# A graph stage in which the centres ride in spare rows, layer two's outputs come out turned, and one more round lies behind the scores

## The chip, the cores and the metric

The kernel runs on one core of a Trainium2 chip. The metric is the time of one execution on the device in microseconds; a kernel is timed several times and its median is given. A profile of one more execution shows what each engine did: PE is TensorE (PEld its weight loads), DVE is VectorE, ACT is ScalarE, POOL is GpSimd, SP issues the DMAs. L with a number is a line of the kernel before.

## The reference, cut to what matters

The whole program has three stages that follow each other: a graph stage (two graph convolutions and a projection), a state-space scan, and a small feed-forward stage. The change lies in the graph stage alone.

There are 16 graphs (`B`) of 512 nodes with 32 features. Four sort orders of the nodes (Morton and Hilbert keys of their coordinates) give each node four windows of 10 neighbours. A graph convolution is:

```python
gf = concatenate([center, neigh - center])       # per sort order, 10 neighbours each
x16 = stack(per order)[..., perm].reshape(B*N, 10, 256).astype(float16)
qh = x16.reshape(B*N, 10, 8, 32)                  # eight heads of 32
attn = softmax(einsum(qh, qh) / sqrt(32))         # 10 x 10 for each node and head
fused = (attn @ qh) @ W_lin.T + b_lin             # 64 channels
h = lrelu(instance_norm(W_conv @ fused))          # 32 channels in layer one, 64 in layer two
feats_next = h.max over the 10 neighbours
```

The layer-one result feeds layer two, and both feed a projection `W_conv3`, whose output is normalized and added to `x`.

In the heads that hold only centres all ten rows of a node are equal, so attention leaves them as they are: they add the same vector to all ten outputs of a node. The kernel computes this "centre share" once per node, together with the biases, and the attention only for the four heads of differences.

## The kernel before, in words

The 16 graphs are handled four at a time (`g` = 0 to 3), on 128 partitions. One pass (`at`) is one layer of one such group; there are eight, in the order (0, layer 1), (1, layer 1), (0, layer 2), (2, layer 1), (1, layer 2), (3, layer 1), (2, layer 2), (3, layer 2). A pass has 43 rounds (`gi`), each for 12 nodes of every graph, so that there are 344 rounds. Queries and keys of three nodes lie in a block of 30 out of 32 columns; a round has four such blocks (`j`), four heads (`h`) and four graphs (`b`).

The steps of a block, each an instruction sequence on its own engine:

- `differences` (POOL, L827) writes neighbour minus centre into `DD`, six rounds ahead; every third round four DMAs on SP's queue copy it into the block-diagonal `DX` (L837).
- `scores` (PE, L862 and L869): a mask product over the whole bank, then 16 products into one PSUM bank `s` (two banks).
- `greatest` (DVE, L878) takes the maximum of each row; `expo` (PE L886, ACT L891) subtracts it by a product with an identity and takes the exponential.
- `sums`, `shares` (DVE L898 and L904, POOL L906): the sum, its reciprocal, and the normalized weights in `EN`. `turn` (DVE L912) transposes them in 32 x 32 blocks into `e`.
- `mapped` (PE L931, ACT L936): the differences through the combined weight `W_conv W_lin` into `us`. The weight is split into three bf16 parts `WA[0..2]`, so there are 48 matmuls a round with 128 (layer one) or 256 (layer two) columns. In layer two `us` takes two banks.
- `outputs` (PE L959): `us` and `e` make the convolution's output `h`, with channels on the partitions: 16 matmuls, `us` is the weight operand and 30 columns of `e` move. In layer one four rounds share the one bank `h`, and at the start of each four, one fp32 product of an identity with `hc` (the centre share, ten times over) lays the centre share into the bank (L949). In layer two, two rounds share a bank.
- `reduce`, `rest` (DVE L976, L982, L985): in layer two the centre share is added (L976), then maximum over the neighbours and moments for the normalization. After a pass, `end` normalizes (L1008 to L1021), and after layer two `finish` projects (L1030).

Beside the rounds run the rank comparisons (`rank_step`, PE L556 into a bank tagged `misc`, ACT L557 reads it), up to three a round in the first pass, one or two in the second and fourth, none in the others; and the preparation of the next pass (`prep`), cut into steps of which one or two are done per round: splitting features, the centre share (L682, L683), one-hot matrices (DVE L767) and their products that sort the features (PE L721, bank `pp`), then a store to memory (`dS`) and spread loads (`fs`, `crep`), all on SP's queue.

The order on every engine is written out by hand. The loop of rounds gives each step a lag: in iteration `it`, `expo` works on round `it-1`, `turn` on `it-3`, `scores` on `it`, `reduce` on `it-4`, `greatest` and `mapped` on `it`, `sums` and `shares` on `it-1`, `outputs` on `it-3`. [...] PSUM has eight banks: two for `s`, two for `u` (mapped products), one `h`, one `pp`, two `misc`.

Of the kernel before, what the change touches and what calls it, by code (L numbers as in the profile page):

```python
# [393 lines left out]
def graph_part(nc, tc, cx, I, dram, id32, ones, xt, F0, layernorm_steps, rstd_steps, scan_input):  # L394
# [45 lines left out]
    for L, co in ((1, 32), (2, 64)):  # L440
        WA = [gc.tile([P, 4, 4, co], BF16, name=f"WA{L}_{k}") for k in range(3)]
        WC = gc.tile([P, co // 32, P], F32, name=f"WC{L}")
        for t in (*WA, WC):
            zero(t)
        layers.append((L, co, co // 32, WA, WC, gc.tile([P, 1], F32, name=f"HB{L}")))

# [17 lines left out]
    for b in range(4):  # L464
        cols = slice(32 * b, 32 * b + 32)
        for j in range(2):
            nc.sync.dma_start(out=W3[cols, j, cols], in_=I["wc3T"][32 * j:32 * j + 32])
        nc.sync.dma_start(out=W3[64 * (b % 2):64 * (b % 2) + 64, 2 + b // 2, cols], in_=I["wc3T"][64:128])
# [22 lines left out]
    for t in (*DD, *EN):  # L491
        zero(t)

# [7 lines left out]
    def weights(L, co, npair, WA, WC, HB):  # L501
# [20 lines left out]
        for k in range(3):  # L522
            for b, rb in enumerate(rows):
                nc.scalar.copy(WA[k][rb, :, b], pw[rb])
            if k == 2:
                break
# [5 lines left out]
        for b in range(4):  # L532
# [3 lines left out]
        wt4 = wp.tile([64, P], F32, name=f"wtr{L}")  # L536
        nc.scalar.copy(
            wt4.rearrange("p (r o) -> p r o", o=co), wt.unsqueeze(1).to_broadcast([64, P // co, co])
        )
        pb = kps.tile([P, 1], F32, tag="w", name=f"pb{L}", bufs=2)  # L540
        nc.tensor.matmul(pb, lhsT=wt4, rhs=bl, start=True, stop=True)
        nc.scalar.copy(HB, pb)
# [84 lines left out]
    ps_s = cx.enter_context(tc.tile_pool(name="gps_s", bufs=2, space=PSUM))  # L627
# [8 lines left out]
    def later_tile(n):  # L636
        return ps_1.tile([P, D], F32, tag="misc", bufs=2, name=f"kd{n}")
# [5 lines left out]
    def prep(g, layer, early=False):  # L643
# [11 lines left out]
        pf = ps_1.tile([P, 4, P], F32, tag="misc", bufs=2, name=f"pf{key}")  # L655
# [14 lines left out]
        def share():  # L670
# [8 lines left out]
            hc = wk.tile([P, npair, D], F32, tag="hc", name=f"hc{key}")  # L679
            for pr in range(npair):  # L680
                ph = ps_1.tile([P, D], F32, tag="misc", bufs=2, name=f"ph{key}_{pr}")
                nc.tensor.matmul(ph, lhsT=WC[:, pr], rhs=c32, start=True, stop=True)  # L682
                nc.scalar.activation(hc[:, pr], ph, AF.Identity, bias=HB)  # L683
                yield
            made[key][2] = hc

        made[key] = [None, None, None]
# [4 lines left out]
        later = []  # L692
# [150 lines left out]
    def begin(at):  # L843
# [5 lines left out]
        mxo = wk.tile([P, npair, D], F32, tag="mxo", name=f"mxo{key}")  # L849
        stats = wk.tile([P, npair, nst, 6], F32, tag="stats", name=f"stats{key}")  # L850
# [63 lines left out]

    def mapped(at, gi):
# [3 lines left out]
        d = DD[slot]  # L919
        us = sm.tile([P, NJ, 4 * co], F32, tag="us", name=f"us{at}_{gi}", bufs=4)  # L920
        u = None
        nj = NJ // npair
        for j in range(NJ):
# [4 lines left out]
            for k in range(3):  # L928
                for h in range(4):
# [3 lines left out]
                        start=(jj == 0 and k == 0), stop=(k == 2), skip_group_check=True,  # L933
# [4 lines left out]

    def outputs(at, gi):
        key, co, npair, WA, hc, per = state[at][:6]  # L940
        us, e = live.pop(("us", at, gi)), live.pop(("e2", at, gi))
        slot = gi % per
        if slot == 0:
            live["h", at] = ps_1.tile([P, npair, per * NQ], F32, tag="h", name=f"h{at}_{gi}")
            if npair == 1:

                f0 = gi * NG
                nn = min(f0 + per * NG, D) - f0
                nc.tensor.matmul(  # L949
                    live["h", at][:, 0, :nn * K].rearrange("p (n j) -> p n j", j=K), lhsT=id32,  # L950
                    rhs=hc[:, 0, f0:f0 + nn].unsqueeze(2).to_broadcast([P, nn, K]), start=True, stop=False,
                    skip_group_check=True,
                )
        h = live["h", at]
        for j in range(NJ):
            for b in range(4):
                pr, r = divmod(b * co, P)
                q0 = slot * NQ + j * QB
                nc.tensor.matmul(  # L959
                    h[r:r + co, pr, q0:q0 + QB], lhsT=us[:, j, b * co:(b + 1) * co],  # L960
                    rhs=e[:, 4 * j + b, :QB], start=npair > 1, stop=True, skip_group_check=True,
                )
# [3 lines left out]
    def reduce(at, gi):  # L966
        key, co, npair, WA, hc, per, mxo, stats = state[at]
# [5 lines left out]
        hs = h[:, :, :nn * K].rearrange("p r (n j) -> p r n j", j=K)  # L973
        if layers[order[at][1]][0] == 2:
            t = sm.tile([P, npair, per * NG, K], F32, tag="hs", name=f"hs{at}_{gi}", bufs=1)
            nc.vector.tensor_tensor(  # L976
                t[:, :, :nn], hs, hc[:, :, f0:f0 + nn].unsqueeze(3).to_broadcast([P, npair, nn, K]), ALU.add,
            )
            hs = t[:, :, :nn]

        def greatest_of():
            nc.vector.tensor_reduce(mxo[:, :, f0:f0 + nn], hs, AX.X, ALU.max)  # L982

        def moments(pr):
            nc.vector.bn_stats(stats[:, pr, gi // per], hs[:, pr].rearrange("p n j -> p (n j)"))  # L985

        if npair == 1:
            greatest_of()
            moments(0)
        else:  # L990
# [10 lines left out]
    def end(at):  # L1001

        g, layer = order[at]
        key, co, npair, WA, hc, per, mxo, stats = state.pop(at)
# [814 lines left out]
```

## Time and profile before

| | us |
|---|---|
| median of three runs | 2255.77 |
| lowest and highest | 2254.24, 2265.24 |
| profiled execution, its own time | 2259.84 |
| span of its instructions | 2258.1 |
| first exponential to the last (344 rounds) | 114.1 to 1291.8 |

| engine | busy us | share of the span | instructions |
|---|---|---|---|
| PE | 2058.6 | 91% | 40533 |
| PE weight loads | 1272.5 | 56% | 40586 |
| DVE | 1792.6 | 79% | 3972 |
| ACT | 1132.6 | 50% | 2066 |
| POOL | 833.6 | 37% | 913 |

Busy time is the union of an engine's instructions, and the modelled end of a matmul overlaps the next one's start. So what a step costs PE is read from start to start in the timeline. "Issue" is idle time for which the profile shows no semaphore. A stretch of time can be cut into windows, and the busy time of each engine asked for in each; this is how the passes are compared.

### The profile page before, as it was taken

What the parts mean: (1) busy time and instruction counts of PE and PEld (TensorE: products, weight loads), DVE (VectorE), ACT (ScalarE), POOL (GpSimd) and SP (SyncE); (2) the same over time, 40 slices, a digit from 0 to 9 for tenths busy, and PEclk for the clock granted to TensorE, in tenths of its full rate; (3) what the DMA queues carried; (4) which work ended last, traced back from release to release, by engine and by line L of the source; (5) the groups of instructions that cost most, each with busy time, mean ns of one, the idle gap of its engine ahead of it and who ended that gap; (6) DMA issues with size and microseconds to landing.
All of it is one profiled execution on the core that took longest, in us unless ns stands there. A gap on an engine that the chain in (4) does not pass through costs nothing. (4 is left out here: it accounts for less than half of the span.)

```text
span 2258.1 us, 91857 instructions
## 1 busy us (share of the span) xinstructions
PE 2058.6 (91%) x40533; PEld 1272.5 (56%) x40586; DVE 1792.6 (79%) x3972; ACT 1132.6 (50%) x2066; POOL 833.6 (37%) x913
## 2 busy tenths in 40 slices
PE   5599898999888998889999969988999999999998
PEld 2255555777456775567777734445465564656443
DVE  8488797999988999989999964397968668685554
ACT  5686577556666554445555523343545445353521
POOL 2156656556556565565555400021112111020210
PEclk9899999999999999999999979999999999999999
DMA  1323233142242321422311122211221312113210
GB/s 45 78 65 79 53 74 73 42 87 49 52 88 47 75 61 41 90 50 62 74 36 43 31 63 61 85 58 44 86 75 38 103 47 75 66 47 94 52 38 19
DMA packets 126395, 138.25 MB, mean 61 GB/s; under 512 B 21051, under 2 KB 84261, under 8 KB 125997
## 3 DMA queue, kind: packets, MB, share of 16 engines
q1 hardware_dynamic: 125997, 132.37, 23.1%
q8 instruction: 319, 5.23, 1.0%
q14 instruction: 79, 0.65, 0.1%
HBM read 77.02 MB, written 12.85 MB: 40 GB/s over the span
## 5 line engine op out<-in xcount | busy, mean ns | idle before, releaser
L906 POOL TENSOR_TENSOR EN<-e,rz 128x480 f32<-128x480 f32 x344 | 342.5, 996 | 500.8 <-DVE rz L904 415.1
L931 PE MATMUL u<-WA,DD 128*32 128x128 bf16 (+1 forms) x16512 | 412.7, 247 | 29.1 <-issue 28.3
L936 ACT COPY us<-u 128x512 f32<-128x512 f32 x516 | 302.1, 587 | 153.3 <-PE u L931 137.8
L931 PEld LDWEIGHTS <-DD 128*32 128x32 f16 x16512 | 337.7, 97 | 52.5 <-issue 50.9
L891 ACT ACTIVATE e<-s,smc 128x480 f32<-128x480 f32 x344 | 227.7, 662 | 255.3 <-PE s L886 222.9
L827 POOL TENSOR_TENSOR DD<-fs,crep 128x480 f16<-128x480 f32 (+2 forms) x344 | 349.7, 1017 | 0.0
L959 PEld LDWEIGHTS h<-e,us 128*32 128x32 f32 (+1 forms) x11008 | 244.9, 125 | 136.0 <-issue 68.9
L959 PE MATMUL h<-e,us 128*32 128x30 f32 (+1 forms) x11008 | 278.1, 210 | 32.8 <-issue 15.0
L1393 POOL TENSOR_TENSOR ssq<-ssq,sq 128x512 f32<-128x512 f32 x56 | 79.5, 1419 | 580.4 <-ACT sq L1392 580.4
L878 DVE TENSOR_REDUCE c<-s 128x16 bf16<-128x480 f32 x344 | 220.6, 641 | 85.2 <-PE s L869 81.5
L1200 PE MATMUL ppg<-hT,wing 128*128 128x512 f32 x512 | 239.9, 612 | 0.0
L1213 DVE SCALAR_TENSOR_TENSOR cyh<-ppch,t_conv_w,cyh 128x496 f32<-128x496 f32 (+2 forms) x192 | 137.5, 716 | 119.8 <-ACT cyh L1207 115.3
L1200 PE MATMUL ppch<-hT,winch 128*128 128x512 f32 x512 | 230.9, 593 | 0.7 <-ACT gs L1288 0.7
L912 DVE STREAM_TRANSPOSE e<-EN 128x512 f32<-128x512 f32 x344 | 224.7, 653 | 0.0
L898 DVE TENSOR_REDUCE z<-e 128x16 f32<-128x480 f32 x344 | 219.6, 638 | 0.4 <-ACT e L891 0.4
L557 ACT ACTIVATE sgn<-kd 128x512 bf16<-128x512 f32 x256 | 153.1, 598 | 50.2 <-PE kd L556 35.0
L869 PEld LDWEIGHTS <-DD 128*32 128x32 f16 x5504 | 80.7, 96 | 157.5 <-issue 134.3
L767 DVE TENSOR_SCALAR oh<-it,rank 128x512 bf16<-128x512 f16 x512 | 156.4, 366 | 9.3 <-PE pp L721 9.3
L869 PE MATMUL s<-DX,DD 128*32 128x120 f16 x5504 | 141.8, 221 | 19.0 <-DMA DX<-DD 14.6
L1200 PEld LDWEIGHTS ppch<-hT,winch 128*128 128x128 f32 x512 | 94.3, 190 | 110.8 <-issue 102.1
L1200 PEld LDWEIGHTS ppg<-hT,wing 128*128 128x128 f32 x512 | 95.1, 193 | 102.6 <-issue 98.9
L886 PE MATMUL s<-c,idb 128*128 128x480 bf16 x344 | 130.0, 378 | 6.0 <-DVE c L878 2.7
(368 smaller groups left out, 2991.2 us busy)
## 6 DMA issues: line engine op xcount, KB each, us to landing
DX<-DD SPq DMA_DIRECT2D x456, 90.0 KB
wing<-in_in_proj SPq DMA_DIRECT2D x64, 256.0 KB
winch<-in_in_proj SPq DMA_DIRECT2D x64, 256.0 KB
wo<-in_out_proj SPq DMA_DIRECT2D x64, 256.0 KB
crep<-dC SPq DMA_DIRECT2D x128, 64.0 KB
dS<-so SPq DMA_DIRECT2D x32, 256.0 KB
fs<-dS SPq DMA_DIRECT2D x128, 64.0 KB
wincB<-in_in_proj SPq DMA_DIRECT2D x8, 256.0 KB
```

What stands on the lines that cost most here:

```text
L767: nc.vector.tensor_scalar(oh[:, j], it2, rank[:, c, m, 4 * g + b:4 * g + b + 1], None, ALU.is_equal)
L827: nc.gpsimd.tensor_tensor(d[:, :, m0 - n0:n1 - n0], win, crep[:, :, m0:n1].unsqueeze(3).to_broadcast([P, 4, n1 - m0, K]), ALU.subtract,)
L869: nc.tensor.matmul(s[rh, j * 4 * QB:(j + 1) * 4 * QB].rearrange("p (b q) -> p b q", b=4), lhsT=d[:, h, c0:c0 + 32], rhs=dx[:, h, :, c0:c0 ...
L878: nc.vector.tensor_reduce(c, live["s", at, gi].rearrange("p (i q) -> p i q", q=QB), AX.X, ALU.max, negate=True)
L891: nc.scalar.activation(e, s.rearrange("p (i q) -> p i q", q=QB), AF.Exp, scale=smc)
L898: nc.vector.tensor_reduce(z, e, AX.X, ALU.add)
L906: nc.gpsimd.tensor_tensor(en[:, :, :QB], e, rz.unsqueeze(2).to_broadcast([P, NI, QB]), ALU.mult)
L912: nc.vector.transpose(e.rearrange("p i q -> p (i q)"), en.rearrange("p i q -> p (i q)"))
L931: nc.tensor.matmul(u[rh, jj], lhsT=d[:, h, c0:c0 + 32], rhs=WA[k][:, h].rearrange("p b o -> p (b o)"), start=(jj == 0 and k == 0), stop=(k ...
L936: nc.scalar.copy(us[:, j - jj:j + 1], u)
L959: nc.tensor.matmul(h[r:r + co, pr, q0:q0 + QB], lhsT=us[:, j, b * co:(b + 1) * co], rhs=e[:, 4 * j + b, :QB], start=npair > 1, stop=True, ...
L1200: nc.tensor.matmul(pp, lhsT=w[:, k], rhs=hT[:, k], start=(k == 0), stop=(k == 3))
```

## The change

- The centre share is stored turned, one row of all channels per node, in memory (`hT`). A new step `centres` loads, for every round, the rows of its nodes into row 30 of the 32-row blocks of `us`, by one DMA on SP's queue (two in a pass's last round). Row 30 was spare. In `EN` the spare column 30 is filled once, at the start, with an indicator of which queries belong to which node (`own_node`); `turn` makes it a row, so that `outputs` adds the centre share by its own product. The product L949 and the addition L976 are gone.
- Layer two's `outputs` swaps its operands: `e` is the weight (32 columns), 64 columns of `us` move, and the output has queries on the partitions. `reduce` transposes the bank on DVE (`ht`) ahead of the same maximum and moments.
- Layer one's `mapped` uses one fp32 weight in place of three bf16 parts: 16 matmuls a round. A new step `widen` on ACT copies the round's differences from fp16 to fp32 for it.
- `s` has three banks, `misc` one.
- One more round lies behind the scores: `expo`, `sums`, `shares` lag by 2, `mapped` by 1, `centres` by 2, `turn` and `outputs` by 4, `reduce` by 5, `rest` by 6.

The diff, cut to its core:

```diff
-        WA = [gc.tile([P, 4, 4, co], BF16, name=f"WA{L}_{k}") for k in range(3)]
+        WA = [gc.tile([P, 4, 4, co], dt, name=f"WA{L}_{k}") for k, dt in enumerate(((F32,), (BF16,) * 3)[L - 1])]
...
+    own_node = kp.tile([P, NB], F32, name="own_node")
+    nc.gpsimd.memset(own_node, 1.0)
+    for base, cm, step in ((0, 1, -32 - K), (K - 1, -1, 32 + K)):
+        nc.gpsimd.affine_select(
...
+    for n in (1, 2):
+        nc.gpsimd.tensor_tensor(own_node[:, 0:1], own_node[:, 0:1], own_node[:, n:n + 1], ALU.add)
+    for en in EN:
+        nc.gpsimd.tensor_copy(en[:, :, QB:QB + 1], own_node[:, 0:1].unsqueeze(1).to_broadcast([P, NI, 1]))
...
-    ps_s = cx.enter_context(tc.tile_pool(name="gps_s", bufs=2, space=PSUM))
+    ps_s = cx.enter_context(tc.tile_pool(name="gps_s", bufs=3, space=PSUM))
...
-        return ps_1.tile([P, D], F32, tag="misc", bufs=2, name=f"kd{n}")
+        return ps_1.tile([P, D], F32, tag="misc", bufs=1, name=f"kd{n}")
...
-            for pr in range(npair):
-                ph = ps_1.tile([P, D], F32, tag="misc", bufs=2, name=f"ph{key}_{pr}")
-                nc.tensor.matmul(ph, lhsT=WC[:, pr], rhs=c32, start=True, stop=True)
-                nc.scalar.activation(hc[:, pr], ph, AF.Identity, bias=HB)
+            hT = dram.tile([D, 4 * co], F32, name=f"hT{key}")
+            nch = 4 // npair
+            for c0 in range(0, 4, nch):
+                ph = ps_1.tile([P, nch, 4 * co], F32, tag="misc", bufs=1, name=f"ph{key}_{c0}")
+                nc.tensor.matmul(
+                    ph, lhsT=id32, rhs=HB.unsqueeze(1).to_broadcast([P, nch, 4 * co]), start=True, stop=False,
...
+                for c in range(nch):
+                    nc.tensor.matmul(
+                        ph[:, c], lhsT=c32[:, (c0 + c) * P:(c0 + c + 1) * P],
+                        rhs=WC.rearrange("p r k -> p (r k)"), start=False, stop=True, skip_group_check=True,
...
+                hc = wk.tile([P, nch, 4 * co], F32, tag="hc", name=f"hc{key}_{c0}", bufs=1)
+                nc.scalar.copy(hc, ph)
+                def keep_share(c0=c0, hc=hc):
+                    nc.sync.dma_start(
+                        out=hT[c0 * P:(c0 + nch) * P].rearrange("(c p) o -> p c o", p=P), in_=hc
...
+    def widen(at, gi):
+        if order[at][1]:
+            return
+        slot, c1 = at_piece(at, gi)
+        d = wk.tile([P, 4, NQ + 2], F32, tag="d32", name=f"d32{at}_{gi}", bufs=2)
+        nc.scalar.copy(d, DD[slot][:, :, c1:c1 + NQ + 2])
...
-            for k in range(3):
+            for k in range(len(WA)):
                 for h in range(4):
                     rh = slice(32 * h, 32 * h + 32)
                     nc.tensor.matmul(
                         u[rh, jj], lhsT=d[:, h, c0:c0 + 32], rhs=WA[k][:, h].rearrange("p b o -> p (b o)"),
...
+    def centres(at, gi):
+        hT = state[at][4]
+        us = live["us", at, gi]
...
+        at_30 = us[QB:QB + 32 * (NB - 1) + 1:32]
+        nc.sync.dma_start(
+            out=at_30[:, :whole], in_=hT[f0:f0 + whole * NB].rearrange("(j n) o -> n j o", n=NB)
...
     def outputs(at, gi):
...
-                nc.tensor.matmul(
-                    live["h", at][:, 0, :nn * K].rearrange("p (n j) -> p n j", j=K), lhsT=id32,
-                    rhs=hc[:, 0, f0:f0 + nn].unsqueeze(2).to_broadcast([P, nn, K]), start=True, stop=False,
...
+                rb = slice(32 * b, 32 * b + 32)
+                if npair == 1:
+                    q0 = slot * NQ + j * QB
+                    nc.tensor.matmul(
+                        h[rb, q0:q0 + QB], lhsT=us[:, j, b * co:(b + 1) * co],
+                        rhs=e[:, 4 * j + b, :QB], start=True, stop=True, skip_group_check=True,
+                    )
+                else:
+                    nc.tensor.matmul(
+                        hv[rb, :, slot, j], lhsT=e[:, 4 * j + b],
+                        rhs=us[:, j, b * co:(b + 1) * co].rearrange("p (c o) -> p c o", c=2),
...
     def reduce(at, gi):
...
-            nc.vector.tensor_tensor(
-                t[:, :, :nn], hs, hc[:, :, f0:f0 + nn].unsqueeze(3).to_broadcast([P, npair, nn, K]), ALU.add,
...
+            if nx == 2 * NJ:
+                nc.vector.transpose(ht.rearrange("p c x q -> p (c x q)"), h)
...
-            if at + 1 >= len(order) or gi < 4 or order[at + 1] == (order[at - 1][0], 1):
+            if at + 1 >= len(order) or gi < 5 or order[at + 1] == (order[at - 1][0], 1):
...
-    for it in range(len(blocks) + 5):
+    for it in range(len(blocks) + 6):
...
-        do(expo, 1)
+        do(expo, 2)
...
-        do(turn, 3)
+        do(turn, 4)
         do(scores, 0)
-        do(rest, 5)
-        do(reduce, 4)
+        do(rest, 6)
+        do(reduce, 5)
...
         do(greatest, 0)
-        do(mapped, 0)
-        do(sums, 1)
+        do(mapped, 1)
+        do(centres, 2)
+        do(widen, 0)
+        do(sums, 2)
...
-        do(shares, 1)
+        do(shares, 2)
...
-        do(outputs, 3)
+        do(outputs, 4)
```

Besides, the weight of the projection (`W3`) is laid out in 32-row parts by four DMAs more, the maxima `mxo` are kept by round, and the normalization after a pass (`lrelu_norm`) reads them in two instructions in place of one.

## The prediction

> **What bounds the kernel now.** I first read the page's busy shares and slices: PE and DVE are both at 0.8 to 1.0 of every slice up to some 1300 us, so the graph stage (344 rounds) has no single bound. Then I cut it into its eight passes of 43 rounds at the exponentials' starts and asked for the busy time of each stretch. Columns: length, then busy us (and instructions) of PE, its weight loads, DVE, ACT, POOL, the granted clock, DMA. Passes 1, 2, 4 and 6 are layer one; shown are passes 1 to 4, 6 and 7.
>
> ```profile
> 114.10:257.70 143.60, 128.46 (x4419) 74.49 (x4416) 118.66 (x268) 95.07 (x218) 85.69 (x95) 0.97 0.31 68
> 257.70:398.80 141.10, 126.12 (x4480) 76.19 (x4501) 122.91 (x274) 100.42 (x223) 86.48 (x96) 1.00 0.31 68
> 398.80:550.20 151.40, 148.39 (x4413) 114.25 (x4413) 143.78 (x341) 83.10 (x140) 85.53 (x95) 1.00 0.28 61
> 550.20:699.10 148.90, 131.56 (x4486) 78.52 (x4507) 129.92 (x300) 100.71 (x228) 86.77 (x97) 1.00 0.30 65
> ...
> 850.10:996.10 146.00, 120.14 (x4447) 76.12 (x4447) 130.70 (x301) 59.68 (x102) 87.91 (x97) 0.95 0.30 65
> 996.10:1147.10 151.00, 149.53 (x4415) 115.15 (x4414) 142.07 (x334) 83.69 (x138) 85.41 (x94) 1.00 0.27 61
> ```
>
> Layer two: PE fills 98% and DVE 95%; both are at their limit. Layer one: PE 82 to 90%, DVE 83 to 90%, and neither explains a span that is almost as long. The timeline of PE shows why:
>
> ```profile
> 930.86 0.38 PE L886 MATMUL s<-c,idb 128*128 128x480 bf16 x1
> 931.07 0.37 PE L862 MATMUL s<-mR,mL 128*128 128x480 bf16 x1
> 931.36 0.41 PE L869 MATMUL s<-DX,DD 128*32 128x120 f16 x16
> 931.59 0.85 PE L931 MATMUL u<-WA,DD 128*32 128x128 bf16 x48
> 932.26 0.83 PE L721 MATMUL pp<-oh,F 128*32 128x512 bf16 x12
> 932.91 0.50 PE L959 MATMUL h<-e,us 128*32 128x30 f32 x32
> 933.34 0.38 PE L886 MATMUL s<-c,idb 128*128 128x480 bf16 x1
> ...
> 934.08 0.73 PE L931 MATMUL u<-WA,DD 128*32 128x128 bf16 x39
> 937.02 0.33 PE L931 MATMUL u<-WA,DD 128*32 128x128 bf16 x9 [2.21 <-issue]
> ```
>
> From start to start a layer-one round costs PE 0.21 + 0.29 + 0.23 + 0.67 (mapped products) + 0.65 (a placing step, 16 a pass) + 0.43 (outputs), 1.83 without the placing. Then PE stops for 2.21 us in the middle of a line's matmuls, waiting for nothing that semaphores show. I added the gaps over 0.3 us in which both PE and its loads stood still and that are put down to "issue": 12.3, 7.0, 8.0 and 18.0 us in the four layer-one passes (45 gaps), under 1 us in layer two. In the packet records, 16 KB arrive on the instruction queue (page, part 3: 319 packets, 5.23 MB) every 3.9 us (median, never under 3.3) in layer one; nearly all 45 gaps end 1.2 to 1.7 us after such a packet ended, and each packet starts when PE has just entered the block before it. 16 KB are 256 instructions (81,119 PE records over 319 packets: 254). So layer one, with 208 PE instructions a round, can't go below 208/256 x 3.3 to 3.9 = 2.7 to 3.2 us a round, against 3.28 to 3.46 measured, and it banks no credit in slow rounds. Four stretches of half clock, 20.4 us in all, follow such gaps in layer one.
>
> **The change, part by part.**
>
> *Layer one's mapped products (L931)*: 48 bf16 matmuls become 16 in fp32. An fp32 matmul is two instruction pairs here (L959: 16 in the code, x32 in the trace), so 96 PE instructions become 64. Time: not shown for 32-row fp32 tiles. Lower end 0.43 (L959's 32 pairs, limited by issue); upper end, four tiles beside each other at 1.04/480 us a column (L949's row below): 512 columns, 1.11. I take 239.9/(256 x 512) = 1.83 ns a column (L1200), 0.94 us, as it is in a stream. +0.27 us a round, 172 rounds.
>
> *Centres*: the 44 fp32 matmuls of L949 go, 0.98 us each from start to start (929.49 to 930.47 below): 11 a pass, -10.8 us. So PE's sum in the second pass: 43 x 1.83 + 63 rank compares x 0.33 + 16 x 0.65 + 10.8 + some 3.5 of preparation = 124; after it 43 x 2.10 + 20.8 + 10.4 + 4.5 = 126. PE gains nothing there in work, but its instructions fall by 33 a round to 175: 2.25 to 2.7 us by the fetch bound, under the engines' floors. The gaps should mostly go.
>
> ```profile
> 929.49 1.04 PE L949 MATMUL h<-hc,id 128*128 128x480 f32 x2 [0.91 <-DVE stats L985]
> 930.47 0.46 PE L959 MATMUL h<-e,us 128*32 128x30 f32 x32
> ```
>
> *Widening on ACT*: 172 copies of 488 elements; L936 copies 512 in 0.59, the exponential 480 in 0.66; 0.53 to 0.66, taken 0.57: +24.5 us a pass. ACT goes from 95, 100, 101, 60 to 120, 125, 125, 84. In the first pass three compares a round for eight rounds make ACT the bound: 0.60 + 0.55 + 0.53 + 3 x 0.72 = 3.84 against 3.58 now: +2, and some +2 in the two-compare rounds after it.
>
> *Layer two's outputs (L959)*: now e is the weight (32 columns), 64 columns move, four matmuls at a time: 4 x 64 x 1.83 ns = 0.47, or 0.43 by issue; taken 0.50, against 1.05 (1113.51 to 1114.57). Upper end 1.05. DVE's addition (L976, 634 ns) becomes a transpose of 512 (L912: 653), the rest of the reduction is of equal size, so DVE stays. Its two rounds without preparation:
>
> ```profile
> 1110.36 0.25 DVE L904 RECIPROCAL rz<-z 128x16 f32<-128x16 f32 x1
> 1110.53 0.65 DVE L912 STREAM_TRANSPOSE e<-EN 128x512 f32<-128x512 f32 x1
> 1111.47 0.66 DVE L976 TENSOR_TENSOR hs<-h,hc 128x480 f32<-128x480 f32 x1 [0.29 <-PE h L959]
> ...
> 1116.78 0.25 DVE L904 RECIPROCAL rz<-z 128x16 f32<-128x16 f32 x1
> ```
>
> 6.42 us for two rounds, 0.29 of it a wait for PE: 3.07 a round. PE falls from 3.21 to 2.66, so DVE is next and holds nearly all: of its 7.6, 7.6, 8.9 and 6.9 idle us in the four layer-two passes I take half, -15.5, and +2 for the longer transposes and 12 split normalizations.
>
> *Centre DMAs*: one or two small SP issues a round (352), waiting for ACT's us copy of the round before; behind them on SP stand stores, spreads, key loads and DX. Their cover is the two rounds until outputs. DX's wait for POOL ends 1.9 us into a round and takes 2.5 to 3.3 us of SP's queue (271.82: 3.14), a small issue 0.35 (crep, 1.41 for four), landing 1.5 after issue (fs waiting for dS): 7.0 us after the round's start, where outputs comes 2 x 2.9 + 2.1 = 7.9 after. Hidden by 0.9; in a collision with dS, crep and fs (0.54 + 1.41 + 1.30) late by up to 2.3, 32 times at most. I take a tenth, 8 us, with the next part.
>
> *One misc bank instead of two*: a compare or a preparation step now waits for ACT to read the last one (0.6 to 0.8). Between two compares of a round lie 1.6 us or more of mapped products, so mostly covered; in preparation and at the end of a group about three uses a pass are not. Counted in the 8.
>
> *Third scores bank, later exponential*: expo's wait for DVE's maximum is already 2.7 us in all; scores' wait for ACT's release keeps one round of slack. It gains little by itself. Filling and draining one more round: 0 to 5, taken +3.
>
> *Preparation* starts a round later; its 46 steps, two a round, still fit the 29 or more rounds left, and its new centre products (five matmuls for one, or six for two) are the 1 us a pass counted above. The steps that move a round keep their order against their neighbours on DVE and POOL: nothing.
>
> *Start*: seven tiny POOL steps, four more W3 DMAs, two weight splits fewer: nothing, since DVE's ordering of the nodes covers them; bare, 3 us.
>
> **Sum.** Layer two's DVE reaches 95% of the span where PE is beside it (143.78/151.40). With floors / 0.95 in layer one: first pass 126/0.95 + 4 = 137; second 126/0.95 = 133; fourth (DVE) 130/0.95 = 137; sixth 131/0.95 = 138. That is 545 for 579.6: -34.6. All: -34.6 - 15.5 + 2 + 8 + 3 = -37. The profiled execution took 2259.8 (span 2258.1), 4.1 above the median of 2255.8; from the median: 2219.
>
> [...]
>
> **Rivals.** (a) *The gaps aren't the fetch, or fewer instructions don't shorten it.* Then the -34.6 go: -15.5 + 2 + 8 + 3 = -2.5, and layer one's extra PE and ACT work (2 us a pass, 4 in the first) is partly bare: +5, 2258. For: the fetch interval never shows its cause. Against: 45 gaps at one distance from a packet. (b) *ACT becomes the bound in layer one*: 120 to 125 busy at 0.90 gives 137, 139, 139, 138: 553, then 2227; still faster. (c) *Slower: the centres arrive late behind DX in SP's queue.* Place: outputs' wait for us. If every DX round (115) stalls PE by 0.4 and all 32 collisions by 2: +110 - 45 = 2321. It decides from about 0.4 us a DX round alone. For: only 0.9 us of cover, and faster rounds shrink it. Against: SP now waits for POOL 631 us, so it has the time; a stall lets DVE and ACT catch up. (d) *Four 32-row fp32 tiles don't run together*: 16 x 0.234 = 3.7 us, +2.8 a round, some 2700. Against: L959's fp32 column groups do overlap (32 x 197 ns in 0.46).
>
> **How the numbers follow.** Forecast 0.60, (a) 0.17, (b) 0.08, (c) 0.12, (d) 0.03. The runs of before differ by 0.5% (11 us), so faster by more needs under 2244.5. Most of (b) and the forecast are faster; a part of the forecast's weak end falls to same: faster 0.67, same 0.17, slower 0.16. The forecast's own range is 2185 to 2245: below, floors reached at 0.98 as PE does in layer two; above, layer one's gain halved and the skipped stalls all paid. With (a) and the near part of (c) the range goes to 2266.
>
> **What would show it.** In the profile after: L931 in layer one about 0.94 us a round in two forms, x5504 fp32 pairs; "issue" gaps in layer-one passes under 15 us; fewer 16 KB packets there (29 for 35 a pass); layer-two PE near 85% with DVE at 97%; L959 at 0.5. Wrong, if PE or its loads wait for "DMA us" for more than 15 us, if ACT's busy share in the first four passes passes 93%, or if the gaps stay with fewer instructions.

## The result: 1.1% slower, and the profile after

| | us |
|---|---|
| before, median (lowest to highest) | 2255.41 (2254.24 to 2265.24) |
| after, median (lowest to highest) | 2280.40 (2277.08 to 2283.10) |
| after over before, 95% interval | 1.0107 [1.0076, 1.0138] |
| forecast | 2219 (2185 to 2266) |

The forecast was wrong in its sign: 37 us less were expected, 25 us more came. The profiled execution after the change took 2279.26 us, its span is 2277.6 against 2258.1. The profiled execution before (2259.84) lay 4.4 above its median, the one after 1.1 below, so the spans differ by 19.5 and not by 25.

The same cut as before the change, at the exponentials' starts, says where the 19.5 us of span lie. The table gives each pass's length; passes 1, 2, 4 and 6 are layer one.

| us | first scores | first exponential | 1 | 2 | 3 | 4 | 5 | 6 | 7 | 8 | after the last exponential |
|---|---|---|---|---|---|---|---|---|---|---|---|
| before | 109.3 | 114.1 | 143.6 | 141.1 | 151.5 | 148.8 | 151.0 | 146.0 | 151.1 | 144.7 | 966.4 |
| after | 113.0 | 124.2 | 148.8 | 148.5 | 149.9 | 152.8 | 149.4 | 145.7 | 148.6 | 142.9 | 966.7 |

Ahead of the first exponential lie 10.1 us more, in the passes 8.9 more, behind them nothing. Layer two's passes are each a little shorter (7.5 together). Layer one's first, second and fourth are longer by 5.2, 7.4 and 4.0, where 7, 8 and 12 less were forecast. These three are the passes with rank comparisons; the sixth has none, and did not change, where 8 less were forecast.

Busy time of the passes after the change (length, then busy us and instructions of PE, its weight loads, DVE, ACT, POOL, the granted clock, DMA); shown are passes 1 to 4, 6 and 7:

```profile
124.20:273.00 148.80, 129.95 (x3732) 79.24 (x3726) 117.48 (x264) 113.30 (x257) 85.37 (x94) 0.99 0.30 65
273.00:421.50 148.50, 132.96 (x3795) 81.95 (x3794) 123.01 (x274) 113.89 (x261) 85.57 (x95) 0.99 0.32 69
421.50:571.40 149.90, 134.89 (x4423) 98.55 (x4423) 145.11 (x345) 84.91 (x146) 87.39 (x96) 1.00 0.31 69
571.40:724.30 152.90, 138.59 (x3815) 83.48 (x3803) 131.31 (x305) 115.86 (x267) 85.52 (x96) 0.98 0.29 67
...
873.60:1019.30 145.70, 120.26 (x3758) 79.97 (x3754) 132.27 (x307) 78.77 (x143) 86.31 (x95) 0.98 0.30 69
1019.30:1167.90 148.60, 133.09 (x4423) 96.64 (x4422) 142.94 (x337) 83.40 (x138) 86.83 (x96) 1.00 0.30 70
```

What was promised to the engines has happened. PE has 3732 instructions in the first pass, not 4419. In layer two its busy time fell (from 148.4 to 134.9 us in the third pass), and DVE fills 96 to 97% there. ACT is at 113 of 149, so it isn't the bound. In layer one no engine is full, as before: PE is at 87, 90 and 91% in the first, second and fourth pass, and these passes are longer. What PE waits for is told by its waits in the eight passes (us in total, times, longest). Before the change the largest is this one, ahead of the mapped products:

```profile
PE u L931 <- issue: 28.3, 66, 2.2
```

After the change:

```profile
PE h L1016 <- DVE ht L1042: 30.5, 40, 2.3
PE h L1011 <- DMA us<-hT: 20.4, 18, 2.3
PE kd L566 <- ACT sgn L567: 11.2, 28, 1.5
PE h L1011 <- DVE e L943: 10.6, 9, 1.8
PE h L1016 <- DMA us<-hT: 9.1, 10, 1.8
...
PE kd L566 <- ACT hc L703: 6.5, 4, 3.4
PE u L973 <- issue: 5.9, 11, 0.9
```

(After the change L1011 is layer one's outputs, L1016 layer two's, L973 the mapped products, L566 a rank comparison, L989 the DMA of the centres, L868 DX, L560 and L561 the loads of keys for a rank comparison.) Three things are to be seen. "Issue" ahead of the mapped products, 28.3 us before the change, is 5.9. In its place stand three waits that were 0.2 us or nothing before: for the centres' DMA (29.5 us in both layers), for ACT to read the one misc bank (11.2), and for ACT's `hc` (6.5). And in layer two PE waits 30.5 us for DVE, which is the bound there and costs nothing by itself.

The wait for the centres as it happens after the change, first the timeline of SP's queue (start, length):

```profile
658.61 2.60 SPq L868 DMA_DIRECT2D DX<-DD  x4
661.26 1.16 SPq L560 DMA_DIRECT2D kr<-others  x1
...
664.70 0.33 SPq L561 DMA_DIRECT2D kl<-own  x1
665.13 0.76 SPq L989 DMA_DIRECT2D us<-hT  x1
```

Then the timeline of PE in the same microseconds:

```profile
663.30 1.08 PE L973 MATMUL u<-WA,d 128*32 128x128 f32 x32
664.19 0.83 PE L752 MATMUL pp<-oh,F 128*32 128x512 bf16 x12
667.36 0.46 PE L1011 MATMUL h<-e,us 128*32 128x30 f32 x32 [2.34 <-DMA us<-hT]
```

DX and eight key loads hold SP's queue from 658.6 to 665.0. The centres are issued behind them at 665.13, PE can start 1.5 us after their issue ends, and has stood for 2.34 us by then. This is the longest of 28 such waits. By SP's timeline some 8 of their 29.5 us stand behind a stretch with key loads, some 12 behind one with the preparation's store and spread loads, and some 7 behind DX alone.

### The profile page after: what moved, and what is told of

It reads as the page before. It is cut to its first block, busy times and chain, and to the rows that moved or that the text cites. A ratio compares the mean times of both kernels' runs of the same rounds, so it can differ in the third digit from the quotient of the medians.

```text
span 2277.6 us, 87696 instructions
## 1 busy us (share of the span) xinstructions
PE 2011.9 (88%) x37794; PEld 1219.5 (54%) x37802; DVE 1800.4 (79%) x4000; ACT 1201.9 (53%) x2230; POOL 835.4 (37%) x918
## 5 line engine op out<-in xcount | busy, mean ns | idle before, releaser
L909 DVE TENSOR_REDUCE c<-s 128x16 bf16<-128x480 f32 x344 | 220.5, 641 | 89.1 <-PE s L900 88.3
L973 PE MATMUL u<-WA,DD 128*32 128x256 bf16 x8256 | 261.4, 273 | 5.4 <-issue 4.9
L973 PEld LDWEIGHTS <-DD 128*32 128x32 f16 x8256 | 213.9, 97 | 12.8 <-issue 9.9
L973 PE MATMUL u<-WA,d 128*32 128x128 f32 x5504 | 191.4, 280 | 2.0 <-issue 1.0
L1016 PE MATMUL h<-us,e 128*32 128x64 f32 x5504 | 116.4, 221 | 61.0 <-DVE ht L1042 31.9
L973 PEld LDWEIGHTS u<-WA,d 128*32 128x32 f32 x5504 | 145.2, 112 | 41.9 <-issue 29.9
L900 PEld LDWEIGHTS <-DD 128*32 128x32 f16 x5504 | 81.2, 96 | 157.9 <-issue 125.7
L900 PE MATMUL s<-DX,DD 128*32 128x120 f16 x5504 | 142.4, 221 | 17.8 <-DMA DX<-DD 14.9
```

What stands on the lines that cost most here:

```text
L900: nc.tensor.matmul(s[rh, j * 4 * QB:(j + 1) * 4 * QB].rearrange("p (b q) -> p b q", b=4), lhsT=d[:, h, c0:c0 + 32], rhs=dx[:, h, :, c0:c0 ...
L909: nc.vector.tensor_reduce(c, live["s", at, gi].rearrange("p (i q) -> p i q", q=QB), AX.X, ALU.max, negate=True)
L973: nc.tensor.matmul(u[rh, jj], lhsT=d[:, h, c0:c0 + 32], rhs=WA[k][:, h].rearrange("p b o -> p (b o)"), start=(jj == 0 and k == 0), stop=(k ...
```

## The experiments

Theory F, from the prediction: the fewer instructions of the fp32 products do take the issue gaps away, and the new waits eat it. Theory S: what eats it is SP's queue, the centres late behind DX and the key loads. Theory A: ACT eats it, by the widening and by more that waits for ACT behind one misc bank. Theory L: the extra round and the third scores bank do harm. All kernels are compared with the kernel before on the chip they ran on; the ratio has a 95% interval. Where two experiments are compared, the difference of their ratios is given in us of 2256, with the two half-widths added in squares. Times by pass come from one profiled execution each; the base below alone ran from 2244.9 to 2264.9 us, so a few us of a pass sum are open.

### Two hc buffers

```diff
-  hc = wk.tile(..., tag="hc", bufs=1)
+  hc = wk.tile(..., tag="hc", bufs=2)
-  d = wk.tile(..., tag="d32", bufs=2)
+  d = wk.tile(..., tag="d32", bufs=1)
```

The second line pays for the first in memory. What made this worth a try is a stall in the second pass of the changed kernel: ACT may not write the second half of the centre share until the first is stored, and the store stands on SP's queue. From the timeline of its engines:

```profile
308.21 0.39 SPq L706 DMA_DIRECT2D hT<-hc  x1
310.45 0.59 ACT L703 COPY hc<-ph 128x512 f32<-128x512 f32 x1 [4.75 <-DMA hT<-hc]
311.09 0.38 PE L566 MATMUL kd<-kr,kl 128*128 128x512 bf16 x1 [3.35 <-ACT hc L703]
311.93 0.66 DVE L1033 TENSOR_REDUCE mxo<-h 128x48 f32<-128x480 f32 x1 [6.91 <-PE h L1011]
```

ACT idles 4.75 us behind a DMA, PE's rank comparison 3.35 behind ACT (it shares the misc bank), DVE 6.91 behind PE.

> The changed kernel with two buffers for the turned centre share hc (and one for the widened differences d32, to make room). Theory A (ACT's work and order bound the layer-one passes with rank comparisons): only the second half of a layer-two share stops waiting, nothing else moves: 2270 to 2280. Theory S (what the change put on SP's queue costs the time: ACT's copy of the second half waits for the store of the first, and PE behind it for the one misc bank; once in each of the four passes that prepare a layer-two group, 11.1 us for one round in the second pass): 10 to 20 us less, 2260 to 2270, and no wait of ACT's hc copy for the DMA of hT in the profile.

Measured: 2273.17, 1.0081 [1.0058, 1.0104], 6 us under the change (6 ± 9, not told apart from nothing by the times alone). The time fell into theory A's range. In the trace the second pass is 142.9 for 148.5, and ACT's waits for the store, 9.8 us in three before, are gone. So the stall is real and costs some 5 us by this one trace; it is only a part of what is sought.

### bf16 mapped products, all else kept

```diff
- WA = [gc.tile([P, 4, 4, co], dt, ...) for k, dt in enumerate(((F32,), (BF16,) * 3)[L - 1])]
+ WA = [gc.tile([P, 4, 4, co], dt, ...) for k, dt in enumerate((BF16,) * 3)]
-        do(widen, 0)
```

> The changed kernel with layer one's mapped products as before: three bf16 parts, 48 matmuls a round, no widening on ACT. Theory A: the three passes with rank comparisons get 5 to 9 us shorter each (ACT's work falls by 25 us a pass), the sixth does not change by more than 3, total 2255 to 2265. Theory F (PE's instruction fetch bounds layer one, and fewer PE instructions help more than the copies cost): the gaps put down to issue come back to some 45 us in the layer-one passes and these get no shorter: 2280 or more.

Measured: 2289.7, 1.0148 [1.012, 1.0175]: slower than with fp32 (9 ± 9). Of PE's waits in this kernel's passes (L971 is the mapped products here, L1009 layer one's outputs):

```profile
PE u L971 <- issue: 24.4, 37, 1.6
PE h L1009 <- issue: 22.7, 23, 2.3
```

The issue gaps are back: those over 0.3 us in the whole graph stage sum to 78.6 us (82) against 34.3 (40). In layer one 51.1 us of them end 1.2 to 1.7 us behind the arrival of a 16 KB block on the instruction queue, against 5.2 with fp32. Theory A's widening falls: without it the kernel is no faster. But the test also brings back 32 PE instructions a round, so it does not price the widening alone. Theory F holds for the gaps.

### One round less, two scores banks, two misc banks

The lags, the banks of `s` and the banks of `misc` go back to what they were before; the fp32 products, the turned outputs and the centres stay.

```diff
- ps_s = cx.enter_context(tc.tile_pool(name="gps_s", bufs=3, space=PSUM))
+ ps_s = cx.enter_context(tc.tile_pool(name="gps_s", bufs=2, space=PSUM))
-        return ps_1.tile([P, D], F32, tag="misc", bufs=1, name=f"kd{n}")
+        return ps_1.tile([P, D], F32, tag="misc", bufs=2, name=f"kd{n}")
...
-        do(expo, 2)
+        do(expo, 1)
-        do(turn, 4)
+        do(turn, 3)
...
-        do(mapped, 1)
-        do(centres, 2)
-        do(widen, 0)
+        do(mapped, 0)
+        do(centres, 1)
+        do(widen, -1)
```

> The changed kernel without its extra round and third scores bank: lags as before, two scores banks, two misc banks, the widening one block ahead. Theory A: the rank passes stay as they are, or lose up to 5 us of waiting for the one misc bank; 2270 to 2280. Theory M (one misc bank and one more round cost the time, at the start and in the rank passes): 10 us at the start and some 5 us a rank pass come back: 2252 to 2262.

Measured: 2254.7, 1.0000 [0.9978, 1.0022]. The whole loss against before is gone (24 ± 9 us under the change), and no gain is left. PE's waits in this kernel's passes (L917 is the product that subtracts the maximum):

```profile
PE s L917 <- DVE c L909: 39.6, 89, 0.8
PE h L1011 <- DMA us<-hT: 32.0, 20, 4.1
...
PE h L1016 <- DVE ht L1042: 9.1, 11, 1.7
...
PE h L1016 <- DMA us<-hT: 5.7, 7, 1.0
```

With one round less PE waits for DVE's maximum (39.6), with one more for DVE's `ht` (30.5): the order with the third bank seems only to move the wait for DVE to another line. The wait for the centres is still there and longer, 37.7. This kernel is called the base from here on; most of the later runs change one thing in it.

### The widening ahead of the mapped products

```diff
+        do(widen, 0)
         do(mapped, 1)
         do(centres, 2)
-        do(widen, 0)
```

> The changed kernel with the widening placed ahead of the copy of the mapped products in ACT's order; the same work. Theory A: in an ACT-bound round ACT waits about 0.35 us for PE's mapped products after the first rank comparison; the widening now fills this wait, so some 100 rounds get 0.2 to 0.35 us shorter: 2245 to 2262. If ACT's order is not what binds: 2275 to 2285.

Measured: 2272.95, 1.0079 [1.0053, 1.0105]: 6 ± 9 under the change, where theory A expected 2245 to 2262. The first pass is 144.1 for 148.8, the second 151.8 for 148.5. The order on ACT is not what costs.

### bf16 again, on the base

```diff
- WA = [... enumerate(((F32,), (BF16,) * 3)[L - 1])]
+ WA = [... enumerate((BF16,) * 3)]
-    widen(*blocks[0])
-        do(widen, -1)
```

> The kernel with one round less behind the scores (two scores banks, two misc banks) and layer one's mapped products as before (three bf16 parts, no widening). What is left of the change: spare rows with their DMAs, and layer two's turned outputs. Theory F (PE's instruction fetch bounds layer one; the 33 instructions a round less of fp32 are worth more than ACT's copies): 5 to 12 us slower than with fp32, 2259 to 2268, gaps put down to issue back near 70 us. Theory W (the widening on ACT eats the gain): 10 to 15 us faster, 2240 to 2246.

Measured: 2272.36, 1.0061 [1.0041, 1.0082]: the fp32 products are worth 14 ± 7 us here, more than theory F's 5 to 12. The issue gaps of the graph stage are 81.2 us (85) against 42.2 (35) in the base; those of layer one that end 1.2 to 1.7 us behind such a block are 50.7 us (55) against 7.5 (6). So the gaps of the prediction's main term do come and go with the number of instructions.

### One misc bank, on the base

```diff
-        return ps_1.tile([P, D], F32, tag="misc", bufs=2, name=f"kd{n}")
+        return ps_1.tile([P, D], F32, tag="misc", bufs=1, name=f"kd{n}")
```

(The same at the tag's three other tiles.)

> The same kernel with one round less, but one misc bank in place of two; the eighth PSUM bank stays empty. Theory M1 (the one misc bank is what cost the changed kernel most of its loss: comparisons wait for ACT to read the one before, at the start and in the rank passes): 2265 to 2275. Theory M2 (the extra round costs it: filling, and steps that wait one round longer): 2255 to 2260.

Measured: 2273.97, 1.0072 [1.0051, 1.0093]: one bank costs 16 ± 7 us. Of it 10.3 lie in the passes of the two profiled executions, 5.0 in the first and 2.9 in the fourth; the rest lies at the start, which wanders among these kernels (below). Of PE's waits in this kernel's passes:

```profile
PE kd L566 <- ACT sgn L567: 13.6, 31, 1.6
```

In the first rounds, with three comparisons each, the second can't start until ACT has read the first, and the mapped products are not between all of them. PE's timeline after the change:

```profile
126.72 0.61 PE L566 MATMUL kd<-kr,kl 128*128 128x512 bf16 x1
128.58 0.38 PE L566 MATMUL kd<-kr,kl 128*128 128x512 bf16 x1 [1.25 <-ACT sgn L567]
```

What then remains between this kernel and the change is the third scores bank and the extra round: 8 ± 8 us. By the profiled executions it is the filling: from the first scores to the first exponential 11.2 us after the change, 6.3 here, 5.7 in the base, while the passes sum to 1186.6 and 1187.7. So the third bank and the extra round together brought nothing in the passes, and the round costs some 5 us once.

### Without the centres' DMAs, on the base

```diff
-        do(centres, 1)
```

The outputs lack the centre share here; it is still computed and stored.

> The kernel with one round less behind the scores, without the DMAs that load the centre shares into the spare rows (the centre share is left out of the outputs). Theory C (late centres hold PE in layer one: 38 us of waits for DMA us<-hT, up to 4.1 us each): 10 to 25 us faster, 2230 to 2245. If PE only waits there in time that it would lose elsewhere: 2250 to 2257.

Measured: 2230.14, 0.9881 [0.9858, 0.9904], so 27 ± 7 us under the base. Busy time of this kernel's first two passes (columns as above):

```profile
119.50:256.80 137.30, 127.94 (x3717) 79.58 (x3717) 119.22 (x266) 112.77 (x262) 84.16 (x93) 0.99 0.32 71
256.80:389.90 133.10, 125.77 (x3794) 82.07 (x3813) 123.36 (x275) 114.50 (x264) 86.26 (x95) 1.00 0.36 75
```

137.3 and 133.1 against 148.6 and 145.5 in the base. The gain that was forecast exists, and the centres' DMAs take it. This does not yet say whether it is the transfers or their place in SP's queue.

### The DX copies spread over the rounds, on the base

In place of four DX copies every third round, two go out at the end of each round, as long as there are some; with two `hc` buffers and one `d32`.

```diff
+    spread_dx = []
+
+    def next_dx(n):
+        for o, i in spread_dx[:n]:
+            nc.sync.dma_start(out=o, in_=i)
+        del spread_dx[:n]
...
-                nc.sync.dma_start(out=DX[slot][rb, :, b, cols], in_=DD[slot][rb, :, cols])
+                spread_dx.append((DX[slot][rb, :, b, cols], DD[slot][rb, :, cols]))
...
+        next_dx(2)
```

> The kernel with one round less behind the scores, with the four DX DMAs of a piece issued two per round (so that a centre DMA stands behind 1.6 us of them at most and not 3.3), and hc in two buffers (d32 in one). Theory C: most of PE's waits for the centres go, 2235 to 2246. If the lateness has another cause than SP's queue: 2248 to 2256.

Measured: 2270.45, 1.0059 [1.0042, 1.0076], 13 ± 6 over the base: a miss. Of PE's waits in this kernel's passes (L909 is the scores' product with DX here, L1020 layer one's outputs):

```profile
PE s L909 <- DMA DX<-DD: 33.1, 21, 3.6
PE h L1020 <- DMA us<-hT: 6.2, 4, 2.4
```

The centres came in time (layer one's outputs wait 6.2 us for them, 32.0 in the base), and now DX came late (33.1 us). Both are on SP's queue, and here DX stood behind.

### The centres issued by POOL, or by ACT, on the base

```diff
-        nc.sync.dma_start(
+        nc.gpsimd.dma_start(
```

(Twice in `centres`; the other kernel has `nc.scalar` there.)

> The kernel with one round less behind the scores; the centre DMAs are issued from POOL's queue in place of SP's. Theory C (the centres come late because SP's one queue works through DX, spreads and key loads ahead of them, and what is queued behind the centres comes late in turn): POOL has a third of its time free, PE's 38 us of waits for DMA us<-hT go, 2235 to 2246. If the DMAs are late for themselves (their own time to land), or if POOL's part in issuing delays the differences and the shares: 2255 or more.

> The same, from ACT's queue. Theory C: the queue is short, but a small issue took SP 0.73 us, and ACT is busy for 113 to 116 of 145 to 150 us in the rank passes: these get longer by what exceeds the rest, the others shorter: 2240 to 2265. If an issue holds ACT for nothing: 2235 to 2242.

Measured for POOL: 2237.75, 0.9922 [0.9899, 0.9946], 18 ± 7 us under the base and under both kernels of the case. The same DMAs with the same bytes, from another queue: so most of the 27 us is SP's queue, not the transfer. The DMA's line in that kernel (shortest, median and longest ns):

```profile
L989 POOL DMA_DIRECT2D us<-hT x344: 582/583/777, 118.8 to 1274.3; - x172
```

Its longest waits on PE in the passes:

```profile
PE s L917 <- DVE c L909: 43.4, 101, 0.8
PE h L1011 <- issue: 13.7, 10, 2.7
PE h L1011 <- DVE e L943: 12.1, 12, 2.4
...
PE h L1011 <- DMA us<-hT: 0.2, 1, 0.2
```

The longest are for DVE, or for nothing that is shown; of the waits for the centres' DMA, 37.7 us in the base, 0.2 is left. POOL pays 0.58 us an issue, 201.8 us in all, and takes it from its slack.

Measured for ACT: 2281.26, 1.0109 [1.0082, 1.0136], 25 ± 8 over the base and above both ranges. ACT pays 0.69 us an issue, and PE waits for another DMA in its passes (L900 is the scores' product with DX):

```profile
PE s L900 <- DMA DX<-DD: 42.2, 18, 6.6
```

DX is still on SP, and is late there because SP now waits for the centres. Of SP's waits in this kernel's passes (L772 is the spread loads):

```profile
SPq L868 <- DMA us<-hT: 49.0, 33, 4.8
SPq L772 <- DMA us<-hT: 46.4, 21, 4.2
```

These two are 95.4 us in 54 waits; in the base and with POOL SP waits for no centres' DMA. Ahead of 15 of PE's 18 waits for DX, SP had waited for one within the last 8 us. Why SP waits for DMAs that ACT issued is not shown, nor how much of the 25 us this makes.

### POOL and two hc buffers; POOL alone on the change

Both have the centres issued by POOL. The first stands on the base and has the two `hc` buffers besides; the second is the change with nothing else edited.

```diff
-        nc.sync.dma_start(
+        nc.gpsimd.dma_start(
```

> As the one with centres on POOL's queue, with hc in two buffers (d32 in one). Theory S: the second half of a layer-two share no longer waits for the first one's store; with two misc banks it held only ACT: 0 to 8 us less than the one with one hc.

> The changed kernel as it is (one more round, three scores banks, one misc bank), with the centre DMAs issued from POOL's queue. If the losses add up (queue 17 to 25 us, one misc bank 19, extra round some 6): 2256 to 2264. If in the changed kernel the late centres were covered by its extra round: 2272 to 2282.

Measured: on the base 2234.51, 0.9905 [0.9882, 0.9929], the fastest that was run of those that compute the whole output; its distance to the kernel without the second buffer (4 ± 8) is not settled. On the change itself: 2257.4, 1.0009 [0.9991, 1.0027], 22 ± 8 us under the change. So the queue costs about as much in the change as on the base, and the losses add up, as the first of the two theories had it.

The passes, as far as they matter:

| us | first scores | first exponential | 1 | 2 | 4 | 6 | all eight |
|---|---|---|---|---|---|---|---|
| before | 109.3 | 114.1 | 143.6 | 141.1 | 148.8 | 146.0 | 1177.7 |
| after | 113.0 | 124.2 | 148.8 | 148.5 | 152.8 | 145.7 | 1186.6 |
| base | 109.7 | 115.4 | 148.6 | 145.5 | 150.5 | 146.8 | 1177.4 |
| base, one misc bank | 113.7 | 120.0 | 153.6 | 146.5 | 153.4 | 146.1 | 1187.7 |
| base, no centres | 113.8 | 119.5 | 137.3 | 133.1 | 144.7 | 143.0 | 1148.0 |
| base, centres by POOL | 114.8 | 120.5 | 138.6 | 133.6 | 144.4 | 146.6 | 1152.3 |
| change, centres by POOL | 113.8 | 125.4 | 146.4 | 140.5 | 144.8 | 146.3 | 1171.2 |

Read downwards in the last column: the products, the turned outputs and the omitted additions bring -29.7 us; the centres' DMAs on SP +29.4, one misc bank +10.3, the extra round and third bank -1.1: +8.9 together. Another 10.1 lie ahead of the first exponential: some 5 the extra round, 1.5 that the kernel with one misc bank shows too, and 3.7 later first scores. The first scores lie between 109.7 and 114.8 us in these kernels though nearly all share their start, so whether the change is the cause of these 3.7 stays open.

## Why the prediction was wrong, step by step

**Layer one's passes, "-34.6".** The gaps went with the instructions, and two of the four sizes held. With the centres' DMAs away the passes are 137.3, 133.1, 144.7 and 143.0 where 137, 133, 137 and 138 stood: -21.4 of -34.6. In the first two PE is the fullest engine (127.9 and 125.8 busy; 126 and 126 forecast). That the first came out at 137 is partly luck: the sum had 4 us for ACT in it, and PE waited for ACT 1.8 us there. In the fourth and sixth DVE is as full as PE or fuller: it has 132.5 in both (129.9 and 130.7 before; the forecast took 130 and 131) and fills 92 to 93%, not 95%. PE and DVE wait for each other there (in the sixth PE waits 6.5 us for DVE's statistics, DVE 7.4 us for PE's scores). The gaps obeyed the instruction count: after the change layer one's passes have 22.2 us of issue gaps for 45.3, and of them 5.2 end 1.2 to 1.7 us behind a 16 KB block, for 37.1 before. A pass takes 29 to 30 of the 16 KB packets in place of 34 to 36 (29 forecast). The sign "under 15 us" was missed; what causes the other 17 stays open.

**The mapped products, 0.94 us.** 0.90 from start to start (659.76 to 660.66), beside one another as taken; rival (d) is out.

**The widening, 0.57 us; rival (b).** 0.60 an instruction. ACT's load was set too high all the same: 113, 114, 116 and 79 us after the change for 120, 125, 125 and 84. ACT did not bind a pass: it fills 77% of one at most, and 86% without the centres' DMAs.

**Layer two, "-15.5 + 2".** Without the centres' DMAs -8.3, after the change -7.5. The base, whose layer-two work is the same, shows -12.5, so a few us are open here. PE was freed nearly as said (busy 148.4 to 134.9 in the third pass, 90% of it where 85% was expected; the outputs 0.59 us from start to start, 457.13 to 457.72, where 0.50 was taken of 1.05), and DVE is next. "I take half" of DVE's idle time was too much for three of the passes: without the centres' DMAs they gained 4.2, 2.0, 1.3 and 0.8. DVE's own work grew by 0.8 us a pass on average, of which 0.5 was in the sum; the transpose takes 676 ns where the addition took 634.

**"Filling and draining one more round … taken +3".** Some 5, by the first exponential; 8 ± 8 by the times. That is the upper end that was given.

**"I take a tenth, 8 us, with the next part".** This is the step that failed: centre DMAs and one misc bank together. Measured are some 40: 18 ± 7 to 27 ± 7 for the DMAs on SP's queue, 16 ± 7 for the bank. Forecast and profile lie 56 us apart (-37 and +19.5); by the table of passes 31 of them are this step, 13 layer one's size, 5 layer two's, and 7 the start. Three parts of the step's working were wrong:

- The price of an issue. 0.35 us was taken from a small DMA of another shape (`crep`). This one has 12 rows of channels and costs SP twice that (columns: shortest, median, longest ns):

```profile
L989 SPq DMA_DIRECT2D us<-hT x344: 683/715/821, 123.4 to 1309.7; - x172
```

  The slack was computed as 0.9 us; 0.37 more an issue, and two or three of them in a row, take most of it or all.
- The collisions. They were counted with `dS`, `crep` and `fs`, 3.25 us, 32 times at most. The eight key loads of the rank comparisons are behind the same DX on the same queue (661.26 to 665.0 above: 3.8 us), and were named in the text but not put into the sum. Some 8 of the 29.5 us of waits stand behind them, and in the base some 17 of 37.7; the rest stand behind DX, the store and the spread loads, which the sum had but called hidden. Nor does a wait cost what it lasts: the sixth pass waits longest, 8.2 us, and became no shorter when POOL issued the centres, while the second and fourth (2.9 and 5.5 us of waits) became 8 shorter each. In the base one such stretch held three rounds' centres back. Its timeline of SP, then of PE:

```profile
381.40 3.06 SPq L868 DMA_DIRECT2D DX<-DD  x4
384.50 0.53 SPq L560 DMA_DIRECT2D kr<-others  x1
...
388.60 0.33 SPq L561 DMA_DIRECT2D kl<-own  x1
389.04 2.37 SPq L989 DMA_DIRECT2D us<-hT  x3
```

```profile
391.40 0.59 PE L1011 MATMUL h<-e,us 128*32 128x30 f32 x32 [4.09 <-DMA us<-hT]
```

- The bank. "Between two compares of a round lie 1.6 us or more of mapped products" is true of one pair in a round with three compares, not of all: PE waits 11.2 us for ACT ahead of compares. And the preparation's `hc` shares the bank, so that a wait for a store on SP reaches PE through ACT (6.5 us).

**Rival (c).** Its place, mechanism and side were right: outputs wait for centres behind DX on SP. It got 0.12. The argument against it, that SP waits 631 us for POOL and so has the time, was the error: the time is there, but in front of DX (360 us are left of it after the change), and the centres, which stand behind DX in program order, went out behind it: at 665.13 after a DX that began at 658.61, at 389.04 after one at 381.40. A share of idle time says nothing on how long one DMA has to stand behind another.

**Rival (a).** Fewer instructions did shorten the gaps. Before the change 140 blocks of 16 KB arrive in layer one's passes (34, 36, 35 and 35). Some 100 have no gap over 0.3 us behind them; the 41 gaps behind the others cost 37.1 us; after the change such gaps cost 5.2. The two bf16 runs differ from their partners: 32 more PE instructions in a round of layer one bring 44 and 39 us more of issue gaps, and 9 ± 9 and 14 ± 7 us of time. That the blocks cause the gaps is the author's reading of these distances; no run shows the cause itself.

**The threshold set in the prediction**, more than 15 us of waits for "DMA us", was passed: 29.5.

## What to carry to other kernels

Price a DMA that is added to a queue by the longest row of issues that can stand ahead of it in program order (here DX and eight key loads, 6.4 us from 658.61 on), with the issue time of its own shape (here 0.715 us), and not by the queue's idle share; if the deadline is one or two rounds, look for an engine with slack and an empty queue, and measure it (here POOL's was worth 18 to 22 us, ACT's lost 25 ± 8). A bank taken from a shared tag made neighbouring uses wait for the reader (28 waits of PE, 11.2 us, after the change), so count the uses in the fullest round, not on average. A change with several parts is worth being cut before it is judged: here the gain was real, and 21 us of it were kept in the fastest kernel; three side parts (the centres on SP's queue, the one misc bank, the extra round), none of which it needs, cost more.

## What the runs showed of the hardware

- PE stood still where the profile shows no semaphore that held it. Before the change a 16 KB block (254 instructions: 81,119 records of PE and its loads over 319 packets) arrived on the instruction queue every 3.9 us in layer one (median, never under 3.3), and 41 gaps, 37.1 us, ended 1.2 to 1.7 us behind one. With a third fewer instructions for the mapped products 8 of these gaps are left, 5.2 us.
- The time that an issue held its queue differed with shape and engine: for the centres' 12 rows 0.715 us on SP after the change, 0.69 on ACT and 0.58 on POOL in the runs with the centres there; for a key load on SP 0.33 (median, after the change).
- The same bytes from another queue: moving the centres' issues from SP to POOL was worth 18 ± 7 us of 2255, and PE's waits for the centres' DMA went from 37.7 us to 0.2. On ACT the same step lost 25 ± 8, and SP waited 95.4 us at DX and the spread loads for the centres' DMAs to land.
- After PE had stood for 4.09 us in the base, the granted clock was half for about 3.4 us, so this wait cost more than its length: the next subtraction of a maximum took 0.58 us on PE, the one after it 0.38 at full clock. The base kernel just after the wait shown above, in stretches of 1 us (the granted clock is the number after POOL's):

```profile
392.00:393.00 1.00, 1.00 (x10) 0.22 (x14) 0.00 (x0) 0.39 (x1) 0.00 (x0) 0.50 0.16 41
393.00:394.00 1.00, 1.00 (x21) 0.38 (x17) 0.52 (x1) 0.27 (x1) 0.00 (x0) 0.50 0.64 147
...
395.00:396.00 1.00, 1.00 (x50) 0.78 (x42) 0.72 (x2) 0.45 (x1) 0.84 (x1) 1.00 0.30 73
```
